# Layer 1 attention: the sums over nodes outside a block are handed from block to block in the loop

## The chip, the core and the metric

The kernel runs on one core of a Trainium2 chip. The metric is device time in microseconds (us), the median of three runs. Engines are named as in the profile: PE is TensorE (PEld its weight loads), DVE VectorE, ACT ScalarE, POOL GpSimd, and SP the queue that issues most transfers.

## The reference, cut to what matters

Four graph layers run on 2708 nodes with 128 features and one dense adjacency `A`. The change concerns layer 1 alone:

```python
XW = jnp.matmul(X, W)
s_col = jnp.matmul(XW, a[0, :f])
s_row = jnp.matmul(XW, a[0, f:])
Z1 = jax.nn.leaky_relu(s_row[:, None] + s_col[None, :], negative_slope=0.01)
den = jnp.exp(Z1)
num = jnp.matmul(A, den)
att = jnp.where(num != 0, den / jnp.where(num != 0, num, 1.0), 0.0)
H = jnp.matmul(A, jnp.matmul(att, XW))
```

`exp` of a leaky ReLU is the larger of two exponentials, so `den[i, j] = max(e^r_i e^c_j, e^.01r_i e^.01c_j)`. The kernel does not multiply the whole `den` by `A`. It sorts the columns j by c and cuts them into blocks. For one block most nodes i take the same side of the maximum for all its columns; they enter through two sums over nodes alone, one of `A * e^r` and one of `A * e^.01r`. Only the nodes whose side switches within the block, its own nodes (at most 126), need their weights one by one.

## The kernel before, in words

Nodes lie in T = 22 tiles of 128 rows (the last has 20 rows), the 2708 columns in C = 6 chunks of 512, 512, 512, 512, 384 and 276. One sweep over the adjacency is 24 panels of four tiles by one chunk (`load_panel`, L157, issued by SP at L160), in three rotating buffers (`strip`), while six more tiles stay resident in `res`. `by_panels` (L171) runs such a sweep: at L186 it multiplies each tile by weights and sums in PSUM.

Layer 1 has these stages:

1. **Ranks.** At the end of the second sweep each node has its rank `rk_f` in the order of c. The rows `xwe` (features, r and c) are scattered to `by_rank` in DRAM by rank (`scatter`, L815: 22 indirect transfers from POOL). `c_edge` holds the c at the head of every block of BJ = 64 ranks (NB = 43 blocks), and comparing r with it gives every node its block `blk`.
2. **Third sweep ("pass 3").** DVE builds `lc` (L865 to L876): for every node and every block the two numbers e^r and e^.01r, each zero where the node isn't on that side of the block. That is 86 columns of weights, and the sweep gives `carry`, 86 rows by 2708 columns. Beside it, further work on DVE and PE (L896 to L914) gives each node its slot in its block; POOL scatters the nodes to `by_slot` (22 more indirect transfers), reads `slots` back, and `ranked` and `listed` (L928, L938) prepare g of all columns (`g_row`), the scaled features `xws`, and the weights `lw` (126 own nodes and two carry rows per block, 64 columns each).
3. **The loop** (L1028 on) over two halves h of the node columns (1354 each) and NQ = 22 pairs of blocks q, so 44 iterations. For each block of a pair POOL gathers the 126 own rows of the adjacency into `rows` (L1035, `strip` buffers again, so three iterations deep), and SP copies the block's two carry rows behind them (L1040). PE multiplies `rows` by `lw` into `num` (L1048), the two blocks of a pair to 64 rows of PSUM each, in a wide part of 1024 columns (two PSUM buffers) and a narrow one of 330 (one buffer). `mix` (L962) then makes the weights: ACT takes a logarithm and an exponential (`inv` = 1/num, L966 and L967), DVE one product of `inv` and `num` and two more steps (L970 to L972), and PE multiplies the result by `xws` into `hacc` (L977).
4. Transposes of `mT` and the fourth sweep follow.

Outside the stretches with `manual_schedule`, where the order is that of the source, a scheduler lays down the order of each engine's instructions when the program is built. Each engine's instructions then stand in that order. The loop is laid down by the scheduler in both kernels.

Of the kernel before, what the change touches and what calls it, by code (L numbers as in the profile page):

```python
# [16 lines left out]
P = 128  # L17
# [3 lines left out]
BJ = 64  # L21
KC = 126
OOB = 4095
# [27 lines left out]
def kernel(  # L51
# [28 lines left out]
    NQ = T  # L80
    S = T - RES
    NB = (N + BJ - 1) // BJ
    HALF = N // 2
# [197 lines left out]
    bw = [min(BJ, N - b * BJ) for b in range(NB)]  # L281
# [46 lines left out]
    y2_rows = dram.tile([N, D], F32, tag="y2_rows", name="y2_rows")  # L328
    with tc.tile_pool(name="knn", bufs=1) as knn:
# [223 lines left out]
        with tc.tile_pool(name="keys", bufs=3) as keys:  # L553

            for n, t in enumerate([*range(4, S), *range(4), *range(S, T)]):
# [20 lines left out]
                nc.vector.max(near[:p, t, :], key[:p])  # L576
# [53 lines left out]
    by_rank = dram.tile([N, D + 2], F32, tag="by_rank", name="by_rank")  # L630
    by_slot = dram.tile([P * NB, 3], F32, tag="by_slot", name="by_slot")
# [151 lines left out]
    lw = lwx.tile([P, NB, BJ], F32, tag="lw", name="lw")  # L783
    sums = ExitStack()
    lc_pool = sums.enter_context(tc.tile_pool(name="lc", bufs=1))
    lc = lc_pool.tile([P, T, NB, 2], F32, tag="lc", name="lc")

    with tc.tile_pool(name="rank", bufs=1) as rank:
        def rtile(shape, name, dt=F32):
            return rank.tile([P] + shape, dt, tag=name, name=name)  # L790

        nc.vector.tensor_copy(rr, xwe[:, :, D])
# [3 lines left out]
        def as_row(col, name):  # L796

            ps = mis_tile()
            nc.tensor.transpose(ps[:T, :P], col, ident)
            lines = rank.tile([T, P], F32, tag=name, name=name)  # L800
            nc.scalar.activation(lines, ps[:T, :P], AF.Exp, scale=0.99)
            flat = dram.tile([T, P], F32, tag=name + "_d", name=name + "_d")
            nc.gpsimd.dma_start(flat[:, :], lines)
            return flat

        def on_all(name, flat):
            row = big.tile([P, N], F32, tag="hT", name=name)
            nc.gpsimd.dma_start(row, bass.AP(tensor=flat.tensor, offset=flat.offset, ap=[[0, P], [1, N]]))
            return row
# [12 lines left out]
        zeros = rtile([3 * NB], "zeros")  # L822
        nc.gpsimd.memset(zeros, 0.0)
        nc.gpsimd.dma_start(by_slot.rearrange("(p b) v -> p (b v)", p=P), zeros)
        nc.gpsimd.memset(xws[:, NQ - 1, :], 0.0)
        nc.vector.tensor_copy(xwe[:, :, D + 1], cc)

# [8 lines left out]
        rk_u = rtile([T], "rk_u", U32)  # L836
        nc.vector.tensor_copy(rk_u, rk_f)
        scatter(by_rank, rk_u, xwe)


        grid = [P, T, NB]
# [11 lines left out]

        neg_r = rtile([T], "neg_r")
        nc.vector.tensor_scalar_mul(neg_r, rr, -1.0)
        blk = rtile([T], "blk")
# [4 lines left out]
        with tc.manual_schedule(engines={nc.vector.engine}):  # L861
            for t0, t1 in ((0, 4), (4, half_t), (half_t, T)):
                n = t1 - t0
                ge = rtile([half_t, NB - 1], "ge")
                nc.vector.tensor_tensor(  # L865
                    ge[:, :n, :], c_edge[:, None, 1:NB].to_broadcast([P, n, NB - 1]),
                    neg_r[:, t0:t1, None].to_broadcast([P, n, NB - 1]), op=ALU.is_ge,
                )
                nc.vector.tensor_reduce(blk[:, t0:t1], ge[:, :n, :], AX.X, ALU.add)
                nc.vector.tensor_add(blk_b[:, t0:t1], blk[:, t0:t1], dead[:, t0:t1])  # L870
                blk_g = blk_b[:, t0:t1, None].to_broadcast([P, n, NB])
                iota_g = iota_b[:, None, :].to_broadcast([P, n, NB])
                for side, (op, v) in enumerate(((ALU.is_gt, e_r), (ALU.is_lt, f_r))):
                    sel = rtile([half_t, NB], "sel", BF16)
                    nc.vector.tensor_tensor(sel[:, :n, :], blk_g, iota_g, op=op)
                    nc.vector.tensor_mul(lc[:, t0:t1, :, side], sel[:, :n, :], v[:, t0:t1, None].to_broadcast([P, n, NB]))  # L876
        spread(lc[:, FULL, :, :])
# [11 lines left out]

        place = rtile([T, NB], "place")  # L890
        totals = rank.tile([P, T, NB], F32, tag="first", name="totals")
        for t0, t1 in halves:
            rhs = in_b[:, t0:t1, :].rearrange("p t b -> p (t b)")
            for dst, lhs in ((totals, ones_b), (place, upper_b)):
                ps = mis_tile()
                nc.tensor.matmul(ps[:, : (t1 - t0) * NB], lhsT=lhs, rhs=rhs, start=True, stop=True)  # L896
                nc.scalar.copy(dst[:, t0:t1, :].rearrange("p t b -> p (t b)"), ps[:, : (t1 - t0) * NB])
        for t in range(1, T):
            nc.vector.tensor_add(totals[:, t, :], totals[:, t - 1, :], totals[:, t, :])
        nc.vector.reduce_max(cnt_max, totals[:, T - 1, :], AX.X)  # L900
        nc.vector.tensor_copy(flag, cnt_max)
        nc.vector.tensor_add(place[:, 1:, :], place[:, 1:, :], totals[:, : T - 1, :])
        nc.vector.tensor_mul(place, place, in_b)
        pos = rtile([T], "pos")
        nc.vector.tensor_reduce(pos, place, AX.X, ALU.add)
# [3 lines left out]
        val = rtile([T, 3], "val")  # L909
        for n, v in enumerate((node_oob, e_r, f_r)):  # L910
            nc.vector.tensor_copy(val[:, :, n], v)
        nc.vector.scalar_tensor_tensor(pos, pos, float(NB), blk, op0=ALU.mult, op1=ALU.add)
        pos_u = rtile([T], "pos_u", U32)
        placed = nc.vector.tensor_copy(pos_u, pos).ins  # L914
        r_row = as_row(rr, "g_r")
        nc.gpsimd.dma_start(
            xws[:, : N // P, :], by_rank[: FULL * P, :].rearrange("(q p) d -> p q d", p=P)
        )
        if LAST:
            nc.gpsimd.dma_start(xws[:LAST, FULL, :], by_rank[FULL * P :, :])  # L920
        scatter(by_slot, pos_u, val)

        carry = big.tile([P, N], F32, tag="y", name="carry")
        slots = rtile([NB, 3], "slots")
        g_row = None


        def ranked():  # L928
            nonlocal g_row
            nc.gpsimd.dma_start(slots.rearrange("p b v -> p (b v)"), by_slot.rearrange("(p b) v -> p (b v)", p=P))  # L930
            with tc.issue_after(placed):
                nc.vector.tensor_copy(csort, xws[:, :, D + 1])
            nc.scalar.activation(g_col, csort, AF.Exp, scale=0.99)
            nc.scalar.activation(g_inv, csort, AF.Exp, scale=-0.99)
            g_row = on_all("g_row", as_row(csort, "g_c"))
            nc.gpsimd.tensor_mul(xws[:, :, :D], xws[:, :, :D], g_col[:, :, None].to_broadcast([P, NQ, D]))

        def listed():  # L938
            for h in range(2):
# [6 lines left out]
            for b in range(NB):  # L946
                nc.vector.tensor_scalar(
                    lw[:, b, : bw[b]], g_row[:, b * BJ : b * BJ + bw[b]], slot_e[:, b : b + 1], slot_f[:, b : b + 1],
                    op0=ALU.mult, op1=ALU.max,
                )  # L950

        def end_carry(c, acc):
            evacuate(c, carry[: 2 * NB, cols[c]], acc[: 2 * NB, : cw[c]])
            if c == 2:
                ranked()
# [208 lines left out]
```

## Time and profile before

| what | us |
|---|---|
| median of three runs (1118.23 to 1118.72) | 1118.64 |
| profiled execution, whole | 1121.06 |
| its span on the core | 1119.4 |
| pass 3, first product to last | 445.5 to 547.7 |
| first gather of the loop's rows | 541.9 |
| loop in steady state, one iteration | 4.9 |
| last product into `hacc` starts | 780.4 |

Times in the text are from the start of the span. In the lists that follow, a line gives start and duration in us, engine, source line, operation, output and inputs with their shape, how many instructions were merged, and in brackets how long the engine sat idle before and for whom. A product in f32 stands in the trace as two matmul instructions.

### The profile page before, as it was taken

The page shows a single profiled execution, that of the slowest core. Times are in us where ns is not written, and L with a number is a line of the kernel's source. Part 1 is how long each engine was busy: PE and PEld are TensorE (multiplying, and loading weights), DVE is VectorE, ACT ScalarE, POOL GpSimd, SP SyncE. Part 2 cuts the span into 40 slices and gives each one's busy share as a digit, 9 for nine tenths or more (in the row PEclk, how much of TensorE's full clock was granted, in tenths as well). Part 3 has the DMA queues.
Part 4 walks back from the last instruction along what each step waited for, and adds up shares of the span by engine and source line. Part 5 has one row for each costly group of instructions (what it writes and reads, how often), then busy time and mean ns, then how long its engine had stood idle before and what let it go on. Part 6 is the DMA issues. An engine that isn't in the chain of part 4 may idle for free.

```text
span 1119.4 us, 10743 instructions
## 1 busy us (share of the span) xinstructions
PE 1044.2 (93%) x3495; PEld 494.5 (44%) x3495; DVE 642.7 (57%) x1381; ACT 306.1 (27%) x569; POOL 299.4 (27%) x296
## 2 busy tenths in 40 slices
PE   0899999999999975999799999998999999999997
PEld 0346544444345654333333333333444644465445
DVE  6885549999636679403099999997311212122132
ACT  0000145555202434000165656664110100011000
POOL 4000000000477772772355655660010100000000
PEclk9999999999999995999999999998999999998999
DMA  9996320000576660797545534454475766563754
GB/s 349 354 316 222 125 101 1 1 0 1 178 274 201 184 207 13 230 304 236 164 121 148 176 96 129 164 171 142 150 236 186 227 227 219 173 227 117 263 166 129
DMA packets 110245, 193.89 MB, mean 173 GB/s; under 512 B 14156, under 2 KB 47106, under 8 KB 109926
## 3 DMA queue, kind: packets, MB, share of 16 engines
q1 hardware_dynamic: 91046, 151.12, 40.7%
q0 software_dynamic: 19136, 42.01, 12.0%
q8 instruction: 29, 0.48, 0.2%
q14 instruction: 34, 0.28, 0.1%
HBM read 217.20 MB, written 4.30 MB: 198 GB/s over the span
## 4 chain that ended last, share of the span: by engine, by line
PE 51%; issue 4%; DMA 4%; DVE 2%; POOL 1%; ACT 1%; POOLq 0%; DVEq 0%; ACTq 0%
PE acc L186 32%; PE hacc L977 8%; PE num L1048 8%; DMA rows<-in_adjT,slot_i 2%; DMA part<-in_adjT 1%; PE mis L259 1%; POOL rows L1035 1%; DVE mask L692 1%; PE mis L1110 0%; PE mis L1063 0%; DMA got<-y_rows,where 0%; ACT junk L710 0%; ACT hT L220 0%; PE mis L1076 0%; DVE mask L697 0%
## 5 line engine op out<-in xcount | busy, mean ns | idle before, releaser
L186 PE MATMUL acc<-part,y 128*128 128x512 f32 (+2 forms) x384 | 156.0, 550 | 2.1 <-DMA part<-in_adjT 1.6
L1035 POOL DMA_INDIRECT rows<-in_adjT,slot_i x86 | 120.7, 1404 | 107.9 <-PE num L1048 79.9
L1048 PE MATMUL num<-rows,lw 128*64 128x512 f32 (+2 forms) x516 | 117.0, 558 | 6.7 <-DMA rows<-carry 3.7
L977 PE MATMUL hacc<-err,xws 128*128 128x512 f32 (+3 forms) x264 | 113.6, 567 | 2.2 <-DVE err L972 1.8
L574 PE MATMUL acc<-zT,z 128*128 128x512 f32 (+4 forms) x264 | 106.9, 552 | 0.0
L602 POOL DMA_INDIRECT got<-y_rows,where x88 | 93.0, 1057 | 29.6 <-issue 11.9
L186 PEld LDWEIGHTS acc<-part,y 128*128 128x128 f32 x384 | 70.4, 191 | 64.5 <-issue 53.9
L970 DVE TENSOR_TENSOR err<-inv,num 128x1024 f32<-128x1024 f32 (+1 forms) x88 | 74.5, 856 | 27.1 <-DMA rows<-in_adjT,slot_i 21.0
L966 ACT ACTIVATE inv<-num 128x1024 f32<-128x1024 f32 (+1 forms) x88 | 64.3, 734 | 88.4 <-PE num L1048 86.6
L575 ACT COPY key<-acc 128x512 f32<-128x512 f32 (+3 forms) x132 | 70.2, 534 | 58.1 <-issue 29.8
L392 PE MATMUL acc<-part,y 128*128 128x512 f32 (+2 forms) x192 | 82.4, 582 | 2.2 <-DVE y L233 2.2
L977 PEld LDWEIGHTS hacc<-err,xws 128*128 128x128 f32 (+1 forms) x264 | 47.1, 192 | 80.4 <-issue 41.8
L186 PE MATMUL acc<-part,lc 128*86 128x512 f32 (+2 forms) x192 | 76.2, 553 | 3.3 <-DVE lc L876 2.5
L186 PE MATMUL acc<-part,xs 128*128 128x512 f32 (+2 forms) x192 | 78.6, 552 | 0.1
L972 DVE SCALAR_TENSOR_TENSOR err<-gb,g_inv,err 128x1024 f32<-128x1024 f32 (+1 forms) x88 | 77.1, 918 | 0.0
L536 POOL TENSOR_TENSOR y<-xs,d2inv 128x2176 f32<-128x2176 f32 (+1 forms) x2 | 4.6, 2322 | 264.3 <-ACT d2inv L534 264.3
L186 PE MATMUL acc<-part,mixed 128*128 128x512 f32 (+2 forms) x192 | 75.0, 545 | 0.2 <-DMA part<-in_adjT 0.2
L971 DVE SCALAR_TENSOR_TENSOR err<-err,inv 128x1024 f32<-128x1024 f32 (+1 forms) x88 | 71.8, 857 | 0.0
L574 PEld LDWEIGHTS acc<-zT,z 128*128 128x128 f32 (+1 forms) x264 | 47.0, 186 | 53.8 <-issue 48.4
L220 ACT COPY hT<-acc 128x512 f32<-128x512 f32 (+2 forms) x18 | 9.6, 534 | 220.1 <-PE acc L186 203.2
L967 ACT ACTIVATE inv<-inv 128x1024 f32<-128x1024 f32 (+1 forms) x88 | 67.3, 768 | 2.6
L576 DVE MAX8 near<-key 128x8 f32<-128x2708 f32 (+1 forms) x22 | 65.3, 2970 | 3.4 <-ACT key L575 3.4
(239 smaller groups left out, 1215.5 us busy)
## 6 DMA issues: line engine op xcount, KB each, us to landing
part<-in_adjT SPq DMA_DIRECT2D x102, 1024.0 KB
part<-in_adjT SPq DMA_DIRECT2D x24, 768.0 KB
part<-in_adjT SPq DMA_DIRECT2D x24, 552.0 KB
res<-in_adjT SPq DMA_DIRECT2D x4, 1280.0 KB
got<-y_rows,where POOLq DMA_INDIRECT x88, 3.9
rows<-in_adjT,slot_i POOLq DMA_INDIRECT x86, 5.8
rows<-carry SPq DMA_DIRECT2D x86, 10.6 KB
xws<-by_rank POOLq DMA_DIRECT2D x1, 1365.0 KB, 10.1
```

The lines of the kernel that those rows point to most:

```text
L186: nc.tensor.matmul(accs[c][: lhsT.shape[-1], :w], lhsT=lhsT, rhs=src, start=start, stop=stop)
L392: nc.tensor.matmul(accs[c][:, : cw[c]], lhsT=y[:, i, :], rhs=src[:, : cw[c]], start=first, stop=last)
L574: nc.tensor.matmul(pks[c][:p, : cw[c]], lhsT=z2[:, :p], rhs=zT[:, cs], start=False, stop=True)
L575: nc.scalar.copy(key[:p, cs], pks[c][:p, : cw[c]])
L602: nc.gpsimd.indirect_dma_start(out=got[:p, :], out_offset=None, in_=y2_rows[:, :], in_offset=bass.IndirectOffsetOnAxis(ap=where[:p, t, k : ...
L967: nc.scalar.activation(inv[:p], inv[:p], AF.Exp, scale=-1.0)
L970: nc.vector.tensor_mul(err[:p], inv[:p], num[:p, :w])
L971: nc.vector.scalar_tensor_tensor(err[:p], err[:p], 2.0, inv[:p], op0=ALU.subtract, op1=ALU.mult)
L972: nc.vector.scalar_tensor_tensor(err[:p], gb[:p, col : col + w], g_inv[:p, q : q + 1], err[:p], op0=ALU.max, op1=ALU.mult)
L977: nc.tensor.matmul(haccs[:, o:e], lhsT=xws[:p, q, :D], rhs=err[:p, o:e], start=(q == 0), stop=(q == NQ - 1))
L1035: nc.gpsimd.indirect_dma_start(out=rows[:KC, n, :], out_offset=None, in_=adj_half[:, :], in_offset=bass.IndirectOffsetOnAxis(ap=slot_i[h][ ...
L1048: nc.tensor.matmul(num[n * BJ : n * BJ + bw[b], o:e], lhsT=lw[:, b, : bw[b]], rhs=rows[:, n, c0 + o : c0 + e], start=True, stop=True,)
```

## The change

- **Blocks.** BJ goes from 64 to 62 and NB from 43 to 44. A block's weights `lw` still have 64 columns: two new ones, in front, hold e^r and e^.01r of its own nodes. So the first two rows of a block's `num` are its carry plus the sums over its own nodes, which is the carry of the next block. e^r enters with a minus sign, and the weights become `relu(g * slot_e + slot_f)`.
- **Chains.** The 44 blocks make 11 chains of CH = 4 consecutive blocks. The loop takes the heads of all chains first, then all second blocks, and so on (`block(s)`). A block's carry is thus made 11 steps, five and a half iterations, before it is read. In `mix`, after the product `err = inv * num`, the new function `keep` copies the two rows from `err` to the next block's rows of `carry`: four transfers on SP for each iteration (two blocks, wide and narrow part), 132 in all, since the last block of a chain hands nothing on. `inv` and `err` change roles so that `err` is left as it is: the second and third step of `mix` write `inv`, and `hacc` is made from `inv`. A scale and a bias of `plain` make `inv` one for the two rows.
- **Pass 3** makes sums for the 11 heads alone: 22 columns of weights, padded to 32. The four tiles of a panel go to four groups of 32 PSUM rows (`part_sum`), and one more product per chunk (`sel`) adds the groups and puts the rows in their places. `by_panels` is not used here any more.
- **Order and queues.** DVE, ACT and PE are ordered by hand from the ranks to the end of pass 3. The transfers for `g_r_d`, `gb`, `xws`, `g_c_d` and `g_row` move from POOL's queue to ACT's. The scaling of `xws` moves from POOL (one instruction) to ACT (22), and half of `lw` moves from DVE to ACT. The zeros of `by_slot` are issued by POOL just before the scatter by rank. `by_rank` now has 22 x 128 rows and is filled with zeros by five POOL transfers in layer 0. `rk_u` needs nine more small DVE steps, since ranks are turned to places in the new order.

```diff
-BJ = 64
+BJ = 62
+CH = 4
...
-    NQ = T
+    NCH = NB // CH
+    NQ = NB // 2
...
-    lc = lc_pool.tile([P, T, NB, 2], F32, tag="lc", name="lc")
+    lc = lc_pool.tile([P, T, 32], F32, tag="lc", name="lc")
...
         def ranked():
-            nc.gpsimd.dma_start(slots.rearrange("p b v -> p (b v)"), by_slot.rearrange("(p b) v -> p (b v)", p=P))
-            with tc.issue_after(placed):
-                nc.vector.tensor_copy(csort, xws[:, :, D + 1])
+            nc.scalar.dma_start(xws, by_rank.rearrange("(q p) d -> p q d", p=P))
+            nc.vector.tensor_copy(csort, xws[:, :, D + 1])
+
+        def turned():
+            on_all(g_row, as_row(csort, "g_c"))
             nc.scalar.activation(g_col, csort, AF.Exp, scale=0.99)
             nc.scalar.activation(g_inv, csort, AF.Exp, scale=-0.99)
-            g_row = on_all("g_row", as_row(csort, "g_c"))
-            nc.gpsimd.tensor_mul(xws[:, :, :D], xws[:, :, :D], g_col[:, :, None].to_broadcast([P, NQ, D]))
+            for q in range(NQ):
+                nc.scalar.mul(xws[:, q, :D], xws[:, q, :D], g_col[:, q : q + 1])
...
+        def part_sum(c, i, g, src, rows=slice(None), last=False):
+            if c not in sums_of:
+                sums_of[c] = acc_tile()
+            nc.tensor.matmul(
+                sums_of[c][32 * g : 32 * g + 32, : cw[c]], lhsT=lc[rows, i, :], rhs=src,
+                start=(c, g) not in begun, stop=last,
+            )
+            begun.add((c, g))
+
+        for c in range(C):
+            w = cw[c]
+            for i0 in range(0, FULL, 4):
+                part = load_panel(i0 // 4, c) if i0 < S else None
+                for i in range(i0, min(i0 + 4, FULL)):
+                    src = part[:, i % 4, :w] if i < S else res[:, i - S, cols[c]]
+                    part_sum(c, i, i % 4, src, last=i + 4 >= FULL and (i % 4 or c % GROUPS) > 0)
+                if (c, i0) == (0, 8):
+                    find_places()
...
+            nc.tensor.matmul(ps[: 2 * NB, :w], lhsT=sel, rhs=tot[:, :w], start=True, stop=True)
+            nc.scalar.copy(carry[: 2 * NB, cols[c]], ps[: 2 * NB, :w])
...
-        by_panels(lambda i: lc[:, i, :, :].rearrange("p b s -> p (b s)"), end_carry)
...
         err = pool.tile([P, w], F32, tag=f"err{w}", name="err")
-        nc.vector.tensor_mul(err[:p], inv[:p], num[:p, :w])
-        nc.vector.scalar_tensor_tensor(err[:p], err[:p], 2.0, inv[:p], op0=ALU.subtract, op1=ALU.mult)
+        nc.vector.tensor_mul(err, inv, num[:, :w])
+        if keep is not None:
+            keep(err)
+        nc.vector.scalar_tensor_tensor(inv, err, 2.0, inv, op0=ALU.subtract, op1=ALU.mult)
...
+    def block(s):
+
+        return s % NCH * CH + s // NCH
...
+                        def keep(err):
+
+                            for n in range(2):
+                                b = block(2 * q + n) + 1
+                                if b % CH:
+                                    o = h * HALF + c0
+                                    nc.sync.dma_start(
+                                        carry[2 * b : 2 * b + 2, o : o + w], err[n * (BJ + 2) : n * (BJ + 2) + 2, :]
+                                    )
+
+                        mix(w, q, num, h * HALF + c0, hacc[:, c0 : c0 + w], own, keep)
```

## The prediction

> **What bounds the kernel now.** First the chain of waits (part 4 of the page), then the stretches around layer 1 (mean granted clock, share of the DMA engines), then the loop in order of time.
>
> ```profile
> PE acc L186 32%; PE hacc L977 8%; PE num L1048 8%; DMA rows<-in_adjT,slot_i 2%; DMA part<-in_adjT 1%; PE mis L259 1%; POOL rows L1035 1%; DVE mask L692 1%; PE mis L1110 0%; PE mis L1063 0%; DMA got<-y_rows,where 0%; ACT junk L710 0%; ACT hT L220 0%; PE mis L1076 0%; DVE mask L697 0%
> ```
> ```profile
> core 0: us, PE busy (x) PEld busy (x) DVE busy (x) ACT busy (x) POOL busy (x), PEclk, DMA share, GB/s
> 445.00:548.00 103.00, 101.32 (x270) 40.35 (x270) 27.79 (x97) 4.77 (x13) 55.96 (x54) 0.98 0.76 244
> 548.00:562.00 14.00, 8.87 (x30) 2.99 (x30) 3.60 (x5) 6.34 (x9) 4.55 (x5) 0.88 0.38 106
> 562.00:779.00 217.00, 213.56 (x749) 80.25 (x748) 209.07 (x260) 127.22 (x171) 111.33 (x78) 1.00 0.45 141
> ```
> ```profile
> 643.03 2.50 PE L1048 MATMUL num<-rows,lw 128*64 128x330 f32 x12
> 643.57 1.76 DVE L970 TENSOR_TENSOR err<-inv,num 128x1024 f32<-128x1024 f32 x2
> 643.84 1.17 SPq L1040 DMA_DIRECT2D rows<-carry  x2
> ...
> 645.25 1.63 DVE L971 SCALAR_TENSOR_TENSOR err<-err,inv 128x1024 f32<-128x1024 f32 x2
> ...
> 645.45 2.54 PE L977 MATMUL hacc<-err,xws 128*128 128x512 f32 x6
> ...
> 645.59 1.02 ACT L966 ACTIVATE inv<-num 128x1024 f32<-128x1024 f32 x1 [0.79 <-PE num L1048]
> ...
> 646.65 1.06 ACT L967 ACTIVATE inv<-inv 128x1024 f32<-128x1024 f32 x1
> 646.80 1.75 DVE L972 SCALAR_TENSOR_TENSOR err<-gb,g_inv,err 128x1024 f32<-128x1024 f32 x2
> ```
>
> Pass 3 (first row) is full of PE work, 101 of 103 us. The loop (third row) is full on PE and on DVE at once, 214 and 209 of 217 us. It can be, since PE works ahead: the wide part of `num` of iteration q+1 is multiplied (643.03, behind the narrow part of q), and only then `hacc` of q-1 (645.45). So ACT makes the next `inv` while DVE is still at q. An iteration takes 4.9 us.
>
> [...] the twelve instructions of `num` hold twice the work of the six of `hacc` at the same widths, and both take 2.5 us. For four no line speaks. [...] the order above is that of the built program. [...] the start of the loop, with gaps in PE, has a clock of 0.88.
>
> **Pass 3: the products.** All columns once cost 2 x 2.5 = 5 us by the `hacc` row (1354 columns each). Before, 21 tiles and the few rows make the 101 us. With four at a time, 21 tiles stand in six rounds (five of four, one alone): 30 us; six products of the few rows and the six of `sel` add at most 2 x 5. So 40 us, if four overlap; if they don't, 101 + 5.
>
> **Pass 3: what is late next.** The transfers. All panels after the first three are 13 x 1024 + 4 x 768 + 4 x 552 KB, 19.0 MB. With 1.4 MB for `xws`, 1.4 each for `gb` and `g_row`, and the last 1.1 of the scatter by rank, 24.3 MB cross while PE goes through the sweep. The middle of pass 3 moved, by the view of transfers for 474 to 504 us,
>
> ```profile
> DMA packets 4972, 9.29 MB, mean 310 GB/s; under 512 B 787, under 2 KB 808, under 8 KB 4972
> q1 hardware_dynamic: 3942, 7.84, 78.9%
> q0 software_dynamic: 1030, 1.45, 16.9%
> ```
>
> with 96% of the 16 engines taken: at 310 GB/s 78 us are needed, at the 363 GB/s that layer 0 reached from 20 to 60 us, 67. I take 74. The first strip comes free at about 448: the first product stood at 445.5 before, and comes later by the nine small steps before `rk_u` (0.1 to 0.2 us each by the neighbouring rows), less for a smaller `lc`. The last panel lands at 522. Before, the chain in order of time shows it at 541.7,
>
> ```profile
> 538.73 3.01 DMA part<-in_adjT
> ```
>
> and the first gathers of the loop (541.9) hang on the strips that the last panels free: 20 us won. Both ends: with no other traffic in the way 19.0 MB take 52 us, but then the lists bind: in order of time POOL's scatter by rank ends at 471 (its last issue starts at 469.5), the scatter by slot takes 28 us more (22 issues of 1.0 with 0.3 between), the wait for the last one some 2 and `slots` 4.1 (508.6 to 512.7 before), so 506, a gain of 34. Without overlap of four, a loss of 5.
>
> The other moves here are hidden. ACT now waits in its queue for the scatter by rank (472) before it may issue `xws`, and has 22 scalings (at 0.27 us, the nearest row, 6 us) before it copies chunk 3; PE waits for `csort` at about 484 (as before, 483.5, since `xws` took 10.1 us to land). Both stop PE for less than three strips, some 9 us, take to fill. `lw` needs `slots` (506) and some 6 us on DVE and ACT together (43 steps took 9.65 on DVE alone), so is ready before 522. Without that cover it costs up to 6. POOL's five transfers of zeros stand where POOL was idle (264 us for `d2inv`): nothing.
>
> **The loop: the saves on SP.** SP spends 0.59 us on each small transfer (two in 1.17 above). Four saves and two loads are 3.5 us of 4.9: it fits. The saves wait for DVE's product, though, and what stands behind them on SP waits too. In the built program the order on SP is: loads of iterations 0 to 2, saves of 0, first load of 3, saves of 1, saves of 2, second load of 3, loads of 4 and 5, saves of 3, and so on. The second load of every third iteration stands behind the save of the iteration just before it. Alone that costs: DVE's product ends, two saves and a load (1.8 us), some 2 to landing.
>
> **The loop: PE's order, the main cost.** The scheduler has laid PE's order to that. Before, `hacc` of q-1 stands behind the wide `num` of q+1 all through. Now, at iterations 3, 6, 18, 26 and 29, `hacc` of the iteration just before stands ahead of all of `num` but the first half of one block; at 9, 12, 15, 32, 35 and 38 it stands ahead of all of it. There the chain has no overlap left. From the start of DVE's product of q (643.57) to the wide end of its third step 4.5 us, `hacc` 2.5, the rest of `num` 1.7 (one block alone 0.86, a pair 0.86), to ACT 0.2, ACT 1.02 + 1.06, to DVE 0.05: 11.0 us against 4.9. Where all of `num` is behind, another wide 0.86 and a narrow 0.55: 12.4. That is 5 x 6.1 + 6 x 7.5 = 75.5 us. At eleven further iterations (8, 11, 14, 17 and so on, and the last four) `hacc` of two before stands within `num`: 1.2 to 1.8 us each by the same sum over two iterations, together 15. (At the loop's start before, `hacc` of 0 stood within `num` of 2 in the same way, and DVE's product of 2 followed that of 1 by 5.7 us, 563.16 to 568.87: 0.8 more than 4.9, so the sum isn't too low there.) So 90 us; from 70 (if the pieces overlap by nearly 2 us at each of the eleven places) to 115 (if PE's gaps of 4 us bring the half clock at each of the eleven). Small gaps of the clock I count with 3. DVE's and ACT's own steps keep their shapes: 0. The err buffer (two of each) waits for a save two iterations old: 0.
>
> **The sum.** 1121.06 - 20 + 93 = 1194 for the profiled execution. It stood 2.4 over the median, so 1118.64 - 20 + 93 = **1191**. The forecast's own range: gains 34 to 10, losses 70 to 115, so 1155 to 1224.
>
> **Rivals.** (1) The drained chains cost far less, since DVE's slack and PE's ready halves fill them: 25 to 50 us, so 1124 to 1149. For it: DVE alone went at 4.75 us for a while (578.53 to 583.28), against it: nothing else is in PE's order to fill. (2) Four products in groups of 32 rows don't overlap: 1118.64 + 5 + 93 = 1217, inside the range above. For it: no line shows four; against it: two overlap in full. (3) The other side: the loop keeps its 4.9 us, because PE's order costs nothing where the loads came early, and only pass 3 is left: 1118.64 - 20 = 1099, down to 1085. It decides as soon as all eleven places together cost under 20 us, 1.8 each. Against it: `hacc` needs DVE's third step, and ACT needs the products behind `hacc`. (4) Nothing is handed on in time: a save is read five and a half iterations, 27 us, later; its time is that of the forecast.
>
> **How the numbers follow.** Forecast 0.78, rival 1 0.10 (slower in it all), rival 2 0.05, rival 3 0.07. Slower by over 0.2% (2.2 us; a measurement of this kernel can't tell less) 0.92, within it 0.01, faster 0.07. The range 1150 to 1224 leaves out rival 3 and most of rival 1.
>
> **What would show it.** Right: pass 3 shorter by 10 to 34 us with the DMA share over 0.85 and PE half idle; DVE's products of iterations 3, 6, 9 following the one before by 11 to 12.5 us and the others by 4.8 to 4.9; DVE idle there for ACT, ACT for `num`, PE for DVE's third step. Wrong: a loop under 240 us, or PE busy through pass 3.

## The result and the profile after

The changed kernel takes 1228.21 us (median of four runs, 1224.60 to 1233.38); the kernel before, beside it, 1118.68. The ratio is 1.098, 95% interval 1.094 to 1.102: slower, as forecast, but 37 us above the forecast of 1191 and 4 above its range. The profiled execution takes 1224.60 us, 103.5 more than that of before.

The chain of waits of the changed kernel:

```profile
PE acc L190 23%; PE hacc L1080 5%; PE num L1155 5%; DVE inv L1074 3%; DMA part<-in_adjT 2%; DMA rows<-carry 2%; DVE err L1071 2%; DMA rows<-in_adjT,slot_i 2%; ACT inv L1068 2%; DVE inv L1075 1%; DMA xws<-by_rank 1%; ACT inv L1067 1%; PE mis L263 1%; PE acc L1029 1%; POOL by_rank L831 1%
```

Before, it was PE almost alone. Now it runs through DVE, ACT and `rows<-carry`, the carry loads: the engines take turns. The stretches of layer 1 in the changed kernel (pass 3, the start of the loop, the loop):

```profile
core 0: us, PE busy (x) PEld busy (x) DVE busy (x) ACT busy (x) POOL busy (x), PEclk, DMA share, GB/s
450.00:535.00 85.00, 51.80 (x281) 11.31 (x281) 22.59 (x90) 23.02 (x66) 48.06 (x48) 0.78 0.88 299
535.00:547.00 12.00, 6.57 (x20) 2.85 (x20) 0.11 (x1) 4.59 (x7) 2.11 (x2) 0.67 0.39 97
547.00:877.00 330.00, 254.54 (x762) 96.22 (x763) 207.17 (x259) 133.74 (x174) 100.19 (x80) 0.91 0.31 92
```

The loop's work has stayed what it was (DVE 207 us, before 209); its length has grown from 214 to 330 us, and PE's granted clock is 0.91. From the first to the last of DVE's wide products in `mix` it is 213.8 us before and 329.6 after; this is called "the loop" below. The difference of the two profiled executions, by stage:

| stage | before | after | difference |
|---|---|---|---|
| up to the third sweep's first product | 445.5 | 450.7 | +5.2 |
| from there to the loop's first wide product | 112.9 | 96.2 | -16.7 |
| the loop | 213.8 | 329.6 | +115.8 |
| from its last wide product to the end of the span | 347.1 | 346.3 | -0.8 |

The products follow each other by 4.76 us where nothing is in the way. At iterations 9, 12, 15, 32, 35 and 38 they follow by 13.8 to 15.1 us, at 3, 6, 18, 26 and 29 by 11.6 to 15.4: the eleven places that the prediction named. Iteration 9 in order of time (in brackets how long the engine sat idle before, and for whom):

```profile
606.00 1.63 DVE L1071 TENSOR_TENSOR err<-inv,num 128x1024 f32<-128x1024 f32 x2 [1.97 <-ACT inv L1068]
...
609.09 1.75 DVE L1075 SCALAR_TENSOR_TENSOR inv<-gb,g_inv,inv 128x1024 f32<-128x1024 f32 x2
...
610.42 4.17 PE L1080 MATMUL hacc<-inv,xws 128*128 128x512 f32 x6 [4.14 <-DVE inv L1075]
614.53 4.28 PE L1155 MATMUL num<-rows,lw 128*64 128x512 f32 x20
617.08 1.72 ACT L1067 ACTIVATE inv<-num,plain 128x1024 f32<-128x1024 f32 x2 [10.75 <-PE num L1155]
...
618.70 1.42 ACT L1068 ACTIVATE inv<-inv 128x1024 f32<-128x1024 f32 x2
...
619.78 1.63 DVE L1071 TENSOR_TENSOR err<-inv,num 128x1024 f32<-128x1024 f32 x2 [8.94 <-ACT inv L1068]
```

DVE, PE, ACT and DVE again, each after the other: the loop drains, that is, no engine has work of another iteration left to fill its wait. `hacc` takes 4.17 us here and up to 4.88 at the others of this kind; before it took 2.54. Iteration 3, of the other kind:

```profile
556.41 1.62 DVE L1071 TENSOR_TENSOR err<-inv,num 128x1024 f32<-128x1024 f32 x2
...
557.65 2.45 SPq L1166 DMA_DIRECT2D carry<-err  x4
...
560.15 4.19 SPq L1147 DMA_DIRECT2D rows<-carry  x5
560.83 2.54 PE L1080 MATMUL hacc<-inv,xws 128*128 128x512 f32 x6 [0.66 <-DVE inv L1075]
566.10 5.87 PE L1155 MATMUL num<-rows,lw 128*64 128x512 f32 x16 [2.73 <-DMA rows<-carry]
569.10 1.73 ACT L1067 ACTIVATE inv<-num,plain 128x1024 f32<-128x1024 f32 x2 [12.53 <-PE num L1155]
...
571.80 1.22 DVE L1071 TENSOR_TENSOR err<-inv,num 128x1024 f32<-128x1024 f32 x1 [10.55 <-ACT inv L1068]
```

Here `hacc` has its 2.54 us, but PE then waits 2.73 more for a carry load that SP issued at 560.15, behind four saves, and that is used at 566.10.

The experiments ran on several chips. On those of e5 to e17 the kernel before took 1157 to 1163 us (beside e1 to e4 1122), so from e5 on only stages of runs of one chip are compared; the loop isn't touched by it (213.3 us in e15, 213.8 in the first profile of before).

### The profile page after: what moved, and what is told of

It is laid out like the page before. It is cut to its first block, busy times and chain, and to the rows that moved or that the text cites. A ratio compares the mean times of both kernels' runs of the same rounds, so it can differ in the third digit from the quotient of the medians.

```text
span 1222.9 us, 11124 instructions
## 1 busy us (share of the span) xinstructions
PE 1035.6 (85%) x3519; PEld 481.0 (39%) x3519; DVE 637.5 (52%) x1376; ACT 329.2 (27%) x622; POOL 281.2 (23%) x295
## 4 chain that ended last, share of the span: by engine, by line
PE 37%; DMA 9%; issue 8%; DVE 7%; ACT 3%; POOL 1%; SPq 0%; DVEq 0%; POOLq 0%; ACTq 0%
PE acc L190 23%; PE hacc L1080 5%; PE num L1155 5%; DVE inv L1074 3%; DMA part<-in_adjT 2%; DMA rows<-carry 2%; DVE err L1071 2%; DMA rows<-in_adjT,slot_i 2%; ACT inv L1068 2%; DVE inv L1075 1%; DMA xws<-by_rank 1%; ACT inv L1067 1%; PE mis L263 1%; PE acc L1029 1%; POOL by_rank L831 1%
## 5 line engine op out<-in xcount | busy, mean ns | idle before, releaser
L1155 PE MATMUL num<-rows,lw 128*64 128x512 f32 (+1 forms) x528 | 142.0, 595 | 38.2 <-DVE err L1071 26.8
L1080 PE MATMUL hacc<-inv,xws 128*128 128x512 f32 (+1 forms) x264 | 128.2, 627 | 45.1 <-DVE inv L1075 44.7
L1139 POOL DMA_INDIRECT rows<-in_adjT,slot_i x88 | 108.7, 1235 | 244.7 <-PE num L1155 210.5
L1071 DVE TENSOR_TENSOR err<-inv,num 128x1024 f32<-128x1024 f32 x88 | 71.5, 854 | 148.8 <-ACT inv L1068 148.7
L1067 ACT ACTIVATE inv<-num,plain 128x1024 f32<-128x1024 f32 x88 | 78.1, 913 | 195.8 <-PE num L1155 176.9
L1080 PEld LDWEIGHTS hacc<-inv,xws 128*128 128x128 f32 x264 | 52.6, 214 | 129.1 <-DVE inv L1075 76.0
L1155 PEld LDWEIGHTS num<-rows,lw 128*64 128x64 f32 x528 | 48.8, 144 | 120.0 <-issue 70.0
L1075 DVE SCALAR_TENSOR_TENSOR inv<-gb,g_inv,inv 128x1024 f32<-128x1024 f32 x88 | 77.0, 915 | 0.0
L1074 DVE SCALAR_TENSOR_TENSOR inv<-err,inv 128x1024 f32<-128x1024 f32 x88 | 71.7, 855 | 0.0
L592 DVE FIND_INDEX8 where<-near,key 128x8 uint32<-128x2708 f32 (+1 forms) x22 | 65.4, 2972 | 0.0
```

The lines of the kernel that those rows point to most:

```text
L1067: nc.scalar.activation(inv, num[:, :w], AF.Ln, scale=plain[:, 0:1], bias=plain[:, 1:2])
L1071: nc.vector.tensor_mul(err, inv, num[:, :w])
L1074: nc.vector.scalar_tensor_tensor(inv, err, 2.0, inv, op0=ALU.subtract, op1=ALU.mult)
L1075: nc.vector.scalar_tensor_tensor(inv, gb[:, col : col + w], g_inv[:, q : q + 1], inv, op0=ALU.max, op1=ALU.mult)
L1080: nc.tensor.matmul(haccs[:, o:e], lhsT=xws[:, q, :D], rhs=inv[:, o:e], start=(q == 0), stop=(q == NQ - 1))
L1139: nc.gpsimd.indirect_dma_start(out=rows[:KC, n, :], out_offset=None, in_=adj_half[:, :], in_offset=bass.IndirectOffsetOnAxis(ap=slot_i[h][ ...
```

## Experiments on the loop

In the lists of e1, e2, e3 and e6 the whole loop is laid down by hand (`manual_schedule` on PE, DVE, ACT and SP). L is a carry load (iteration, block), K the saves of an iteration, P products into `num`, H products into `hacc`, W and N the wide and the narrow part.

**e1: all by hand.** SP around iterations 3 to 6 and PE around 9 (the lines taken out are the changed kernel's order):

```diff
-K0 L3.0 K1 K2 L3.1 L4.0 L4.1 L5.0 L5.1 K3 L6.0 K4 K5 L6.1
+L3.0 L3.1 K0 L4.0 L4.1 K1 L5.0 L5.1 K2 L6.0 L6.1 K3
-P8.N H7 H8 P9.W0 P9.N0 P9.W1 P9.W2 P9.W3 P9.N1 P10.W
+P8.N P9.W H7 P9.N P10.W H8
```

> The changed kernel with the loop laid down by hand: on SP the two carry loads of iteration q+3 stand ahead of the saves of q, on PE the wide num of q+1 stands behind the narrow num of q and ahead of hacc of q-1 all through, ACT and DVE keep whole iterations in a row. All saves, loads and steps are kept. Theory (the order on SP and PE makes the drains): DVE's wide products 4.75 to 4.95 us apart all through, 208 to 216 us from the first to the last (329.6 in the changed kernel, 213.8 before), so 1224.6 - 116 = about 1108 us for one execution. Rival (the saves themselves cost it: SP's time, their transfers, or the longer ACT and DVE steps): the loop stays over 280 us, over 1170.

Measured: the loop 226.7 us, 1129.91 in the median of 11 runs, before beside it 1121.79, ratio 1.008 (1.0045 to 1.0116). The loop in the windows and in order of time:

```profile
560.00:786.00 226.00, 217.21 (x761) 80.79 (x762) 206.77 (x258) 140.23 (x172) 95.32 (x81) 1.00 0.45 131
```
```profile
690.90 1.20 ACT L1229 ACTIVATE inv<-num,plain 128x1024 f32<-128x1024 f32 x1 [1.57 <-PE hacc L1255]
691.35 2.50 PE L1223 MATMUL num<-rows,lw 128*64 128x330 f32 x12
...
692.86 1.17 SPq L1212 DMA_DIRECT2D rows<-carry  x2
...
693.77 1.62 DVE L1234 TENSOR_TENSOR err<-inv,num 128x1024 f32<-128x1024 f32 x2
693.78 2.54 PE L1255 MATMUL hacc<-inv,xws 128*128 128x512 f32 x6
...
695.01 2.44 SPq L1239 DMA_DIRECT2D carry<-err  x4
```

With every save and every load in place the loop has lost 103 of its 116 us. So the saves themselves, SP's time for them and the longer ACT steps aren't the cause; the order is. Of the 13 us left, 3.1 stand at the change of halves (9.1 between two products, before 6.0), where this order has PE wait for a copy of `hacc`. The rest lies at iterations such as 8, 9 and 14 (6.3 to 7.5 us). PE and its weight loads wait longer for gathers than before (for `rows<-in_adjT` 3.4 and 11.2 us, before 1.2 and 3.6), but as these waits overlap, their share isn't shown.

**e4: no saves, the scheduler's order.** In the diff `b` of the load is the head of the chain.

```diff
-                        b = block(2 * q + n)
+                        b = block(2 * q + n) // CH * CH
...
-                        mix(w, q, num, h * HALF + c0, hacc[:, c0 : c0 + w], own, keep)
+                        mix(w, q, num, h * HALF + c0, hacc[:, c0 : c0 + w], own)
```

> The changed kernel without the 132 saves, its loop laid down by the scheduler: no sums are handed on, every block reads the carry rows of its chain's head. Theory (saves on SP's queue make the scheduler lay the order that drains): the wide num of q+1 ahead of hacc of q-1 all through as in the kernel before, products 4.75 to 4.95 us apart, loop 208 to 216 us, about 1108 us. Rival (the new mix is slower by itself: ACT's logarithm 1.20 instead of 1.02 us wide, roles of inv and err changed): the loop stays over 280.

Measured: 219.1 us, PE's order that of before but for the first iterations. So it is the saves that make the scheduler lay the order that drains. This run takes two things away at once, the saves' place among the loads on SP and the loads' dependence on them; e11 below takes only the first.

**e2 and e3: one half of the order each.** e2 has e1's orders on PE, ACT and DVE and the changed kernel's on SP; e3 the other way round (the diff of e1, one pair of lines each).

> As e1 in the orders of PE, ACT and DVE, but SP's order is that of the changed kernel: the second carry load of every third iteration stands behind the saves of the iteration just before it. This prices the load's place alone. Theory 'both': at each of the eleven places the load leaves SP 4.3 us after the start of DVE's product of the iteration before (1.26 to its end, four saves and a load of 0.6 each), lands 2.5 later, then 0.65 of num and 2.26 of ACT: 9.8 us against 4.76, so 211 + 11 x 5 = 266 us for the loop, about 1160. If a load lands 5 us after its issue instead, about 295 and 1190. Theory 'PE's order alone' (the loads' place costs nothing once PE is ordered well): below 225, below 1120.

> The other half: the orders of PE, ACT and DVE are those of the changed kernel (hacc of q-1 ahead of num of q at eleven iterations), but SP issues the carry loads of q+3 ahead of the saves of q. This prices PE's order alone. Theory 'PE's order alone': the products at the eleven places stay 11 to 12.4 us apart (12.2 to 13.2 with ACT's order there, logarithms of both parts ahead of the exponentials), loop 295 to 315 us, 1190 to 1210. Theory 'the loads do it': below 240, below 1135. The difference from the changed kernel's 329.6 is what late loads add on top.

Measured: e2 342.5 us, longer than the 329.6 with both orders; e3 333.7, hardly more than the 329.6 to 333.4 of all runs of the changed kernel. Mending one half alone gains nothing; each drains the loop by itself. e2 at iteration 6:

```profile
592.13 1.63 DVE L1234 TENSOR_TENSOR err<-inv,num 128x1024 f32<-128x1024 f32 x2
...
593.38 2.44 SPq L1239 DMA_DIRECT2D carry<-err  x4
...
595.86 3.77 SPq L1212 DMA_DIRECT2D rows<-carry  x5
601.33 3.65 PE L1223 MATMUL num<-rows,lw 128*64 128x512 f32 x6 [9.45 <-DMA rows<-carry]
604.90 3.20 PE L1255 MATMUL hacc<-inv,xws 128*128 128x512 f32 x6
607.59 1.21 ACT L1229 ACTIVATE inv<-num,plain 128x1024 f32<-128x1024 f32 x1 [14.46 <-PE hacc L1255]
...
609.91 1.63 DVE L1234 TENSOR_TENSOR err<-inv,num 128x1024 f32<-128x1024 f32 x2 [12.94 <-ACT inv L1231]
```

17.8 us where 9.8 were expected: the load's issue to its first use took 5.5 us instead of 3.1 (0.6 for SP and 2.5 to landing, the latter an estimate), PE was at half clock after 9.45 idle us (granted clock 0.50 from 601.3 to 605), and ACT's logarithm waited for `hacc` too. That last wait is new in the changed kernel: since `hacc` reads `inv`, and there are two buffers of it, the logarithm of q+1 needs `hacc` of q-1 done. In e1 the same wait stands (1.57, `<-PE hacc`) and costs nothing. PE's order in the changed kernel, bad as it is, would thus be fitted to late loads: `hacc` done first leaves less to do once they land. That is a reading of e2, not tested by itself.

e3 at iteration 9, with the load long landed:

```profile
619.78 1.75 DVE L1247 SCALAR_TENSOR_TENSOR inv<-gb,g_inv,inv 128x1024 f32<-128x1024 f32 x2
621.11 4.88 PE L1255 MATMUL hacc<-inv,xws 128*128 128x512 f32 x6 [4.14 <-DVE inv L1247]
625.92 4.93 PE L1223 MATMUL num<-rows,lw 128*64 128x512 f32 x20
629.13 1.72 ACT L1229 ACTIVATE inv<-num,plain 128x1024 f32<-128x1024 f32 x2 [12.11 <-PE num L1223]
...
631.82 1.63 DVE L1234 TENSOR_TENSOR err<-inv,num 128x1024 f32<-128x1024 f32 x2 [10.29 <-ACT inv L1231]
```

In e3 the places without a long gap on PE (3, 6, 18, 26, 29) take 11.56 us each, near the 11.0 of the prediction; those with 4.14 idle us ahead of `hacc` take 15.13 instead of 12.4. (333.7 includes 11.55 at the change of halves, where the order written out has PE wait for a copy; the changed kernel has about 5 there.)

**e6: keep PE busy in that gap.**

```diff
+                elif k == "F":
+                    for _ in range(8):
+                        nc.tensor.matmul(
+                            nums[key][:, NARROW:], lhsT=xws[:, q, :D], rhs=gb[:, : CW - NARROW], start=True, stop=True
+                        )
```

> e3 with eight further small products (128 x 182, into unused columns of num's narrow buffer, nothing reads them) in PE's order ahead of hacc at iterations 9, 12, 15, 32, 35 and 38, where PE stood idle for 4.14 us before hacc and hacc took 4.88 us. Theory (the idle gap halves the clock, and that was the missing cost): hacc takes 2.54 there and num about 2.0, so the products follow at 11.6 to 12.1 us instead of 15.13, and the loop is 313 to 317 us against 333.7 in e3. Rival (something else slows hacc and num there: the memory, the DMA's writes): unchanged at 15.1, the loop 330 or more.

Measured: the loop 314.3 us, at the six places 12.13 to 12.16. Iteration 9 again:

```profile
687.70 0.78 PE L1230 MATMUL num<-gb,xws 128*128 128x182 f32 x4
688.49 2.54 PE L1261 MATMUL hacc<-inv,xws 128*128 128x512 f32 x6
690.95 4.26 PE L1224 MATMUL num<-rows,lw 128*64 128x512 f32 x20
693.52 1.72 ACT L1235 ACTIVATE inv<-num,plain 128x1024 f32<-128x1024 f32 x2 [9.13 <-PE num L1224]
```

More work on PE, and 19 us less: `hacc` is back at 2.54, and `num` reaches ACT 2.5 us after `hacc` is over rather than 3.1. The half clock after the gap of 4.14 us was worth 3.0 us at each of the six. (In the first profile of the changed kernel the granted clock is 0.59 from 610.4 to 614.6, in e3 0.50 from 621 to 627, here 1.00 from 684 to 696.)

**e11: saves on ACT, the scheduler's order.**

```diff
-                                    nc.sync.dma_start(
+                                    nc.scalar.dma_start(
                                         carry[2 * b : 2 * b + 2, o : o + w], err[n * (BJ + 2) : n * (BJ + 2) + 2, :]
```

> The changed kernel with one word changed: the 132 saves are issued by ACT, SP keeps the carry loads alone, and the scheduler lays down the loop. In the built program hacc of q-1 never stands ahead of all of num of q on PE; at every second iteration it is split around one product of num. Theory (loads behind saves in one queue make the drains): no product later than 9 us after the one before, loop 215 to 255 us. Rival (the saves drain the loop whichever queue they are on, here ACT waits for DVE's product before it can start the next logarithm): over 290 us.

Measured: 278.5 us, between the two, so both were off. The loads still depend on the saves, yet no drain is left over 9.4 us, which points to the shared queue rather than to the dependence. But most iterations alternate between 4.7 and 8. Two things are mixed here, ACT's wait for DVE ahead of a save and a PE order with split `hacc`; their shares weren't separated.

## Experiments on pass 3

**e5, e9, e12, e16: the changed kernel again; e15: the kernel before with a profile.**

> The changed kernel itself once more, on the chip of the next three runs, as their yardstick: the loop's products over 325 to 335 us. It also says how much of the start of the loop (546.9 us in the first profile, 559.5 to 562.3 in three of the kernels with the loop laid down by hand or without saves) comes from the chip rather than from the kernel.

> The changed kernel once more as yardstick for the two runs beside it: loop 325 to 335 us between its first and last product; the start of the loop 95 to 110 us after the first product of the third sweep.

> The changed kernel as yardstick on this chip for the two runs beside it. On a chip without the 30 us stops of ACT that e5 and e9 showed: 95 to 113 us from the first product of the third sweep to the loop's first product, loop 325 to 335.

> The changed kernel beside it. On a quiet chip 95 to 108 us from the third sweep's first product to the loop's first; with the stop some 130.

> The kernel before itself with a profile, on the chip of the next two runs. In e5 to e14 three chips gave 1157 to 1163 us for it instead of 1119 and stops of some 30 us in the changed kernels. If the stop in pass 3 belongs to the chip alone, this profile has it too and its third sweep's first product to the loop's first product takes some 140 us; if it comes only with the changed pass 3, 108 to 118 us as in the first profile (112.9). On a quiet chip: 112 to 114.

Measured: the loop 332.7, 331.1, 331.1 and 333.4 us, and 213.3 in e15: it repeats to about 1%. From the sweep's first product to the loop 132.4, 132.2, 125.7 and 132.3 us, and 126.8 in e15. On these chips ACT stands still at two places. One lies in the second sweep, ahead of pass 3, in every kernel, that of before too. In e15 it keeps PE idle for 29 us:

```profile
358.49 2.08 PE L647 MATMUL mis<-w,hT 128*128 128x128 f32 x8 [29.01 <-ACT hT L733]
```

The other lies in pass 3, and only the changed kernels have it: in each of their twelve profiles from e5 on ACT is idle for 28 to 42 us ahead of a copy into `tot` (the sums of a chunk), at most 15 us in the first profile and in e1 to e4. In e16 (`remote` stands where the trace has nothing that released the instruction):

```profile
539.00 0.58 ACT L1048 COPY tot<-acc 128x512 f32<-128x512 f32 x1 [35.53 <-remote]
```

PE is idle for 33 us there. In e15 no gap of PE in pass 3 is over 6.5 us. At neither place does the profile show what ACT waits for. So the first stop isn't the change's, while the second comes only where the changed pass 3 and these chips meet; what stops ACT, and which of the moves in pass 3 lets it happen, stays open. On the chip of e15 and e16 pass 3 gained nothing: 132.3 against 126.8 (before had taken 112.9 in its first profile; why it takes 14 us more in e15 without a stop in pass 3 isn't shown). On the chip of e1 to e4, where pass 3 is the changed one too, it took 102.9 to 108.4.

**e7 and e13: `xws` earlier** (in e1's kernel). In the first profile of the changed kernel the transfer is late, and so is all that hangs on it; the last panel ends 530.2:

```profile
483.86 17.28 DMA xws<-by_rank
501.14 0.02 issue
501.17 0.19 DVE csort L991
...
525.95 4.21 DMA part<-in_adjT
```

```diff
-            if c == 1:
+            if c == 0:
                 ranked()
```

> e1 with one number changed: the transfer of xws is issued by ACT behind chunk 0's copy to carry and not behind chunk 1's. Theory (the late issue of xws holds PE in front of the transposes of csort, so the strips stay full and the panels stop): the issue at 479 to 481 instead of 487, csort 8 to 12 us earlier than e1's 507.4, the start of the loop 4 to 10 us earlier against e1's pass 3. Rival (DMA alone bounds pass 3, xws only takes bandwidth from the panels): csort earlier but the start of the loop within 2 us.

> The kernel of e7 (loop by hand; xws issued behind chunk 0's copy). Theory (xws's late issue holds back pass 3): csort 8 to 12 us earlier after the sweep's first product than in e12, the loop's first product 4 to 10 us earlier. Rival (DMA alone bounds pass 3): within 2 us of e12.

Measured: after the sweep's first product `csort` came 39.5 us later in e13 and 72.2 in e12, yet the loop began after 127.0 and 125.7; in e7 79.9 against 83.0 (e5), and 133.2 against 132.4. A `csort` 33 us earlier won nothing, so the late `xws` didn't bound pass 3 there. With ACT's stop of some 30 us in these profiles, that says little for a chip without it.

**e8, e10, e14, e17: all together**, with the copy of `hacc` moved and `find_sel` ahead of the sweep.

```diff
-            if c == 0:
-                find_sel()
+        find_sel()
...
+                    if g == NQ:
+                        finish(0)
```

> The changed kernel with the loop by hand as in e1, the copy of the first half's hacc moved behind the next exponentials on ACT (9.1 us between products at the change of halves in e1), xws as in e7, and find_sel ahead of the third sweep (PE waited 6 us for sel). Theory: loop 213 to 224 us, start of the loop 8 to 16 us earlier than e1's, so 10 to 20 us under e1, that is 1107 to 1120 on this scale, and faster than before by up to 1%. Rival (pass 3 is bound by its DMA traffic and nothing is won there): 1122 to 1130, no faster than before.

> The kernel of e8 once more, beside a run of the changed kernel on the same chip, because in e5 to e8 all engines stood still for some 30 us in pass 3. Theory: the third sweep's first product to the loop's first product 84 to 98 us (96.2 in the first profile of the changed kernel, 112.9 before), the loop 213 to 224, so 105 to 125 us under the changed kernel of this chip, and level with before or up to 1% faster. Rival (pass 3 is bound by its traffic): 96 to 105 us for pass 3, 0 to 1% slower than before.

> The kernel of e8 and e10. Theory: pass 3 8 to 16 us shorter than e12's, loop 213 to 224, so level with before or up to 1% faster. Rival: pass 3 as in e12, level with before or up to 1% slower.

> The kernel of e8. Theory (late xws bounds pass 3): pass 3 8 to 16 us shorter than e16's; loop 213 to 224. On a quiet chip level with before or up to 1% faster; where the stop is, 1 to 3% slower as in e10 and e14. Rival (traffic bounds pass 3): as e16 within 2 us.

Measured: loop 221.3, 222.4, 226.2 and 223.6 us; pass 3 to the loop 127.0, 133.2, 119.0 and 129.4, against 132.4, 132.2, 125.7 and 132.3 of the changed kernel beside it. Ratios to before 1.031 (1.029 to 1.034), 1.027 (1.021 to 1.032), 1.023 (1.015 to 1.030) and 1.029 (1.025 to 1.033). That is some 9% better than the changed kernel (1193.55 against 1309.45 beside e17), and still behind before. Stage by stage e17 is behind e15 by 3.8 us ahead of pass 3, 2.6 in it, 10.3 in the loop and 1.6 behind it. No version that was run beats before; all together was not run on a chip without ACT's stop in pass 3.

## Why the prediction was wrong in its size

The direction and the mechanism stood: the eleven places, their two kinds, and `hacc` ahead of `num` as what joins the chain. For the profiled execution it said 1194; it was 1224.6. The loop's sum was 22.8 us short, the gain up to the loop 8.5 too large, the rest 0.8 better. (The median stood another 3.6 above that execution.)

| term | prediction | measured | by |
|---|---|---|---|
| five places of the first kind, at full clock | 30.5 | 33.3 | e3: 5 x (11.56 - 4.9) |
| six of the second kind, at full clock | 45 | 43.5 | e6: 6 x (12.15 - 4.9) |
| half clock at the second kind | in 3 | 14.4 | 87.3 us at the six in the first profile - 6 x 12.15 |
| late carry loads at the first kind | 0 | 8.8 | 66.6 us at the five - 5 x 11.56 |
| all other iterations | 15 | 15.8 | 175.7 - 32 x 4.9, less the 3.1 over 4.9 that before had |
| loop | 93 | 115.8 | |

- **The step that failed first: "Small gaps of the clock I count with 3."** The prediction saw gaps of 4 us coming. That they bring half clock was the author's assumption, and it stood at the end of the range alone. The half clock cost 14.4 (granted clock 0.50 from 621 to 627 in e3). PE's wait for DVE's third step is the same at each of the six places, 4.14 us (4.13 to 4.14 in six profiles), and a slow `hacc` (4.17 to 4.88 us) followed all 36 times, so it belonged in the sum. e6 is the proof: `hacc` 2.54 us, clock 1.00. The drains themselves, sized from before's rows, were right to 0.6 us.
- **"Alone that costs ... 1.8 us, some 2 to landing"** was priced but never added where PE's order drains anyway. (The 2 us were an estimate: before's `by_slot<-zeros`, 64.5 KB, landed 1.9 us after its issue; a landing of the carry loads is not shown.) There the load comes in only after `hacc` is over: 2.73, 1.51, 0, 0.51 and 2.06 us of waiting, partly at a lower clock after it (0.62 from 566.0 to 569.5).
- **ACT's part** was taken over from before: "ACT 1.02 + 1.06". The logarithm now takes 1.20 us, and at the drains the narrow logarithm stands between it and the exponential; this is the 0.6 us by which 11.56 exceeds 11.0. "DVE's and ACT's own steps keep their shapes: 0" was wrong for ACT. At the second kind the same 0.6 is hidden by luck: the products from the end of `hacc` to ACT took 2.5 us in e6, where the sum has 3.3. The instructions by form, before and after:

```profile
L966 ACT ACTIVATE inv<-num 128x1024 f32<-128x1024 f32 x42 | 43.0, 1023 | 46.2 <-PE num L1048 45.5 <-DVE err L972 0.8
```
```profile
L1067 ACT ACTIVATE inv<-num,plain 128x1024 f32<-128x1024 f32 x44 | 52.9, 1203 | 183.4 <-PE num L1155 165.0 <-PE hacc L1080 18.4
L1067 ACT ACTIVATE inv<-num,plain 128x330 f32<-128x330 f32 x44 | 27.4, 623 | 12.4 <-PE num L1155 11.9
```

  With scale and bias from `plain` the wide logarithm takes 1203 ns, without them 1023: 180 more. The narrow one takes 623 against 446: 177 more.
- **Pass 3: "I take 74".** Products packed by four, in the prediction an assumption, did overlap (24 of them in 2.98 to 4.48 us), and DMA is what bounds: PE is busy 52 of 85 us, the DMA engines' share is 0.88. But the traffic moved at 299 GB/s, not at the 328 that 24.3 MB in 74 us need; the last panel is there 79.5 us after the first product. The row of before had shown 310. The gain to the last panel is 541.7 - 530.2 = 11.5 us. It was to land at 448 + 74 and landed at 450.7 + 79.5: of the 8.2 between, 5.5 are the transfers and 2.7 the later start.
- **"POOL's five transfers of zeros stand where POOL was idle ...: nothing."** POOL is idle there, but the DMA engines aren't. The zeros cross while the first panels of layer 0 come in (first line in order of time, second the zeros' queue over the first 28 us: packets, MB, share of the DMA engines):

```profile
14.06 2.68 POOL L591 DMA_DIRECT2D by_rank<-res  x5
q0 software_dynamic: 224, 1.46, 14.6%
```

  At the 382 GB/s of 12 to 18 us, 1.46 MB take 3.8 us, by estimate. The same instruction of layer 0, DVE's second `MAX8`, stands at 166.9 us before and at 170.9 after; the first one stands at 163.4 to 168.1 in all seventeen profiles with the zeros, at 160.9 and 163.0 in the two of before. That fits, but no run leaves the zeros out, and 1.2 us were lost ahead of them (DVE's first use of a panel at 7.85 us instead of 6.61).
- **"PE waits for `csort` at about 484"**: it was 501. ACT reaches the issue of `xws` only behind chunk 1, at 483.9 instead of 472, and the transfer took 17.3 us rather than 10.1. What that cost on a chip without ACT's stop isn't shown.
- **All other iterations** came out right partly by luck: nine of them take 6.7 to 7.4 us, 19.5 more than 4.9 each, while most of the rest go at 4.76.
- **Rivals.** Rival 1 (chains cheaper than they look) and rival 3 (the loop keeps its pace) are out by the gaps themselves, rival 2 by the first profile. Rival 3's loop is nearly what e1 and e4 reach: the order, not the hand-over, is its price. Rival 4 has the forecast's time, and no time here tells it apart.

## What to carry to other kernels

When small transfers that wait for an engine share a queue with loads that feed it, look at the built order of that queue and of PE: here one load behind one late save was enough to have the loop drain at that place (17.8 us at iteration 6 of e2, against 4.76), and mending only one of the two orders was worse than none (342.5 us in e2, against 329.6). When a chain is about to drain, add up PE's idle time in it: a gap of 4.14 us at each of six turns was half clock at each of them (0.50 from 621 to 627 in e3), for `hacc` and part of what followed. Ask of a transfer not only whether the engine that issues it is idle, but whether the DMA engines are. And price an instruction with its operands, not by the row of its simpler form (the logarithm: 1203 ns against 1023).

## What was not expected of the hardware

- PE idle for 4.14 us and then given `hacc`: 4.88 us instead of 2.54. With eight small products in the gap, 2.54. Shorter gaps went both ways. One of 1.97 us left `hacc` at 2.54 in the changed kernel, one of 1.83 us at the end of before's loop did not, with PE busy at full clock until then:

```profile
776.82 4.37 PE L977 MATMUL hacc<-err,xws 20*128 20x512 f32 x6 [1.83 <-DVE err L972]
```

  The granted clock is 0.56 from 776.8 to 781.2. In e15, the same kernel, the same gap of 1.83 us left it at 2.53. In the other seventeen profiles 2.35 to 2.44 us stand ahead of the last `hacc`, and it took 2.54 in seven of them and 3.6 to 4.24 in ten. So here the length of a gap of 1.8 to 2.4 us doesn't tell whether `hacc` behind it is slow.
- A transfer of two rows of 5.4 KB takes SP 0.56 us to issue, and its use on PE followed 5.5 us after the start of the issue in e2, with the DMA engines' mean share between 0.08 and 0.16 for the last three of these. At iteration 3 of the changed kernel it followed after 5.95 us, with a share of 0.11 for the last 2.65. What the load waits for isn't shown.
- Four products with 32 columns of weights side by side do overlap: 24 instructions of 512 columns took 2.98 to 4.48 us in the first profile of the changed kernel. One after the other they would take 24 x 0.43 = 10.3, an estimate from `hacc` there: its weight loads of 561.37, 561.80 and 562.23 follow each other by 0.43.
